# One VectorE operation a step in the wide waves, and three pieces of work moved between GpSimd, ScalarE and VectorE

## The chip, the cores and the metric

The kernel runs on one core of a Trainium2 chip. The metric is the device time of one execution in microseconds (us). A core has five engines with queues of their own: TensorE (PE) multiplies matrices into PSUM, VectorE (DVE) and ScalarE (ACT) compute on SBUF and PSUM, GpSimd (POOL) computes on SBUF, and SyncE (SP) issues nearly all DMAs here.[...]

## The reference

A block of three residual stages over x, 2048 tokens by 1024 channels in fp32. The middle stage convolves along the channel axis with a kernel that is built from a state-space model; the first and the last are the same gated feed-forward with weights of 4 bits:

```python
def _dequant(qweight, scales, qzeros, g_idx):   # groups of 128 rows
    ...
    return (w.astype(scales.dtype) - z[g_idx].astype(scales.dtype)) * s

x = L0_attn_u
x = x + 0.5 * _L0_ffn_ref(_layernorm(x, axis=-1), ...)   # silu(x@Wg) * (x@Wu) @ Wd
x = x + _L0_attn_ref(_layernorm(x, axis=-1), ...)        # y = causal conv(x, K) + D*x
x = x + 0.5 * _L0_ffn_ref(_layernorm(x, axis=-1), ...)
```

Wg and Wu are 1024 x 2752, Wd is 2752 x 1024; the 2752 inner channels are 21 tiles of 128 and a half tile of 64.

## The kernel before

**Jobs.** The tokens form four blocks of 512. A feed-forward of one block is a job; there are eight, numbered 0 to 7: `JOBS = [(0, 1), (1, 1), (0, 3), (1, 3), (2, 1), (3, 1), (2, 3), (3, 3)]`, each a block and a stage (1 the first feed-forward, 3 the last). A job has an up stage of 64 steps and a down stage of 44 steps.

**Up stage** (`gate_up`). A step is a wave of output tiles and one group of 128 input rows. Waves 0 to 4 are wide: three tiles of Wg and three of Wu, six units, steps 0 to 39. Waves 5 to 7 are narrow: four units in steps 40 to 55, and four and the half tile's unit in steps 56 to 63. A unit is one PSUM bank of 128 x 512 and takes two matmuls a step (L744), one with the low part of x (fp16, `xTl`) and one with the high part (`xTh`), in the same int8 weights cast to fp32r. After each step the bank is multiplied by the ratio of two groups' scales (`rat`), in place: even units on ScalarE (L714), odd ones on VectorE (L716), with some of unit 1's on ScalarE in jobs 0 and 1. The next step's matmuls on that bank wait for this. At the end of a wave, `gated` takes silu on ScalarE (L771), the product on VectorE (L774), and the high and low parts of h on GpSimd (L776, L778).

**Down stage** (`down`). The same for Wd, two halves of 22 steps, four banks (`po`), matmuls on L813. The half tile of 64 rows comes last in a half, at step 21; `gated_half` makes it: h of it stands in partitions 64 to 127, its high part stays there and its low part goes to partitions 0 to 63 of the same tile `hb`. `split` inside it is a generator of two GpSimd operations (L793, L795), which hooks pull at down steps 1 and 2.

**Hooks.** Everything else is attached to steps: `at(up, s, f)` and `at(dn, d, f)` call f when step s or d is written. Which step an instruction is written in, and its dependences, are what the Tile scheduler starts from; it then orders each engine's queue by its own estimate of times. `in_order_of_writing(f, engines)` pins the instructions of f, on the named engines, behind what was written on them before. `in_pieces` spreads the yields of a generator over a list of steps, pinned on VectorE; the last step takes all that is left.

**Preparing the next job.** While a job runs, the x of the next one gets its moments (`moments`, L187 and L188: two statistics of 512 columns and one aggregation for each of four tiles of 128 tokens), an inverse square root by three Newton rounds (`guess`, `deviations`, L195 to L213), and its normalization. From job 1 on, the normalization is `normalize` (L257), in place in x, eight pieces of 512 columns; in the down stage GpSimd splits x into parts and DMAs turn them. In jobs 3 and 4 the next x comes fresh from the input, so its moments lie there: all of them are written at up step 44, the Newton rounds at 45. In jobs 2, 5 and 6 the next x has just been convolved in the same job and saved to HBM (`save`, L1449, up step 28), and its moments are at 27. In jobs 2 to 6 the normalizations are written at up steps 46, 48, 50 and so on to 60. Job 1 prepares later and isn't touched by the change, and job 0 prepares job 1's x in its down stage in another way.

**Job 0** makes the int8 weights as it goes. For wave w, VectorE splits packed words into bytes in six pieces (L567, L569, L571), GpSimd copies eight int8 rows sets (L600), SP writes each to HBM (L601), and the weights of a step are read back (L676, four steps ahead) and cast three steps ahead, on GpSimd (L692) or, for some steps of job 0, on ScalarE (L690). `first_weights` sets the steps: wave 2's split starts at up step 3, with the fetch of wave 3's words and zero points three steps later.

**The opening.** Block 0's x is turned by TensorE, one chunk of 128 channels at a time (`first_turn`); chunk c is what step g = c of each wave needs. Chunks 0 to 4 go straight from PSUM: ScalarE casts the high part (L1589), VectorE subtracts for the low part (L1590). Chunks 5 to 7 are copied to SBUF by ScalarE (L1593), and GpSimd makes both parts (L1594, L1595).

Of the kernel before, what the change touches and what calls it, by code (L numbers as in the profile page):

```python
# [9 lines left out]
F32 = mybir.dt.float32  # L10
# [8 lines left out]
ALU = mybir.AluOpType  # L19
AX = mybir.AxisListType  # L20
ET = mybir.EngineType
# [20 lines left out]
LIFT = 2.0**20  # L42
# [13 lines left out]
def macaron_s4_kernel(  # L56
# [31 lines left out]
    nc = tc.nc  # L88
# [52 lines left out]
    def in_order_of_writing(f, *engines):  # L141

        start = len(nc.cur_bb.bb.instructions)
        got = f()
        written = list(nc.cur_bb.bb.instructions)
        for e in engines:
            last = next((i for i in reversed(written[:start]) if i.engine == e), None)
            for ins in written[start:]:
                if ins.engine == e:
                    if last is not None:  # L150
                        tc.add_manual_dep(
                            ins,
                            last.name,
                            mybir.DependencyInfo(
                                mybir.DependencyClass.NoSync, mybir.DependencyReason.DATA
                            ),
                            reason="order of writing",
                        )
                    last = ins
        return got  # L160
# [15 lines left out]
    def moments(b, k):  # L176
        for _ in moments_by_tile(b, k):
            pass

    def moments_by_tile(b, k):  # L180

        name = f"{b}_{k}"
        stats = small.tile([P, NT, 2, 6], F32, tag="stats", name=f"stats_{name}")
        mv = small.tile([P, NT, 2], F32, tag="mv", name=f"mv_{name}")
        for t in range(NT):
            for i in range(2):
                nc.vector.bn_stats(stats[:, t, i, :], x[b][t][:, bass.ts(i, 512)])  # L187
            nc.vector.bn_aggr(mv[:, t, :], stats[:, t, :, :].rearrange("p a s -> p (a s)"))  # L188
            yield
        guess(b, k, mv)  # L190
# [383 lines left out]
    def split(w):  # L574
        raw, z = packed[w]
        even = t4(f"even_{w}").bitcast(I32)[:, : width_of(w)]
        return signed_bytes(w, raw, even, z)
# [57 lines left out]
    def first_weights(up, dn, at):  # L635

        for w in range(1, len(WAVES)):
            s0 = (0, 3, 8 * w - 15)[min(w, 3) - 1]  # L640
            steps = (0, 1, 2, 2, 3, 3) if w == 1 else range(6)
            in_pieces(at, [(up, s0 + d) for d in steps], lambda w=w: split(w))
            copies = {1: (2, 2, 3, 3, 3, 3, 3, 3), 2: (3, 3, 4, 4, 6, 6, 7, 7)}
            if 1 < w < len(WAVES) - 1:
                both = lambda w=w: (fetch(w + 1), fetch_zeros(w + 1))
                at(up, s0 + 3, lambda both=both: in_order_of_writing(both, ET.SP))
            for k, d in zip((0, 2, 4, 6, 1, 3, 5, 7), copies.get(w, (3, 3, 4, 5, 6, 6, 7, 8))):
                at(up, s0 + d, lambda w=w, k=k: dequantize(w, k))
        s0 = len(STEPS) - 12
        when = lambda n: (up, s0 + n) if n < 12 else (dn, (5 * (n - 12)) // 6)  # L650
        for n in range(6 * 8):
            k, j = divmod(n, 8)
            a, rt = divmod(k, 3)
            if j == 0:
                at(*when(max(0, n - 7)), lambda a=a, rt=rt: fetch_down(a, rt))
                steps = [when(max(0, n - d)) for d in (4, 3, 3, 2, 1, 0)]
                in_pieces(at, steps, lambda a=a, rt=rt: split_down(a, rt))
            at(*when(n), lambda a=a, rt=rt, j=j: dequantize_down(a, rt, j))
# [122 lines left out]
    def gated_half(j, p):  # L781

        last = rat[:, 2 * WIDE, GK - 1 :]
        low, high = slice(0, HALF), slice(HALF, P)
        g = gpool.tile([P, TB], F32, tag="g", name=f"g_{j}_half")
        nc.scalar.activation(g[high], p[low], AF.Silu, scale=last[low])
        hf = hfpool.tile([P, TB], F32, tag="hf", name=f"hf_{j}_half")
        nc.vector.scalar_tensor_tensor(hf[high], p[high], last[high], g[high], ALU.mult, ALU.mult)
        both = hpool.tile([P, TB], F32R, tag="h", name=f"hb_{j}")
        h[WIDE] = (both,)  # L790

        def split():
            nc.gpsimd.tensor_copy(both[high], hf[high])  # L793
            yield
            nc.gpsimd.tensor_tensor(both[low], hf[high], both[high].bitcast(F32), ALU.subtract)  # L795

        half_split[j] = split()

    half_split = {}
    yT = {}  # L800
# [607 lines left out]
    def fast():  # L1408
        for j, (b, k) in enumerate(JOBS):
            prev = JOBS[j - 1] if j else None  # L1410
            after = JOBS[j + 1] if j + 1 < len(JOBS) else None
            up, dn = {}, {}

            def at(hooks, s, f):
                hooks.setdefault(s, []).append(f)
# [65 lines left out]
            if after:  # L1481
                ab, ak = after
                if ak == 1:
                    at(up, 55 if j == 0 else 6, lambda: load_x(ab, rows_of(u, ab)))
                    if j == 0:
                        steps = [(dn, d) for d in range(3, 8)]
                        in_pieces(at, steps, lambda: moments_by_tile(ab, 1))
                        newton = lambda: deviations(ab, 1, LIFT)
                        at(dn, 8, lambda: in_order_of_writing(newton, ET.DVE))
                    else:  # L1490
                        both = lambda: moments(ab, 1)
                        at(up, 44, lambda: in_order_of_writing(both, ET.DVE))
                        at(up, 45, lambda: deviations(ab, 1, LIFT))
                an = {}

                pool = j == 0

                def anorm(t):
                    an[t] = normalized(ab, t)

                o = 9 if j == 0 else 0
                turns = {}

                def turning(t):
                    if t not in turns:
                        turns[t] = [], []
                        turns[t] += (turn_by_dma(ab, t, turns[t][1]),)
                    rest = turns[t][1] or turns[t][2:]
                    next(rest[0], None)

                for t in range(NT if j else 0):
                    late = (12, 13) if t == NT - 1 else (13, 17)
                    for half in range(2):
                        piece = lambda t=t, half=half: normalize(ab, t, half)
                        piece = lambda piece=piece: in_order_of_writing(piece, ET.DVE)
                        at(*((dn, 3 * t + half) if j == 1 else (up, 46 + 4 * t + 2 * half)), piece)
                    for d in (1, 2, 3, 5, 6, 7, 9) + late:
                        piece = lambda t=t: turning(t)
                        piece = lambda piece=piece: in_order_of_writing(piece, ET.Pool, ET.SP)
                        at(dn, 2 + 9 * t + d, piece)  # L1520
                for t in range(0 if j else NT):
                    at(dn, o + 1 + 4 * t, lambda t=t: anorm(t))
                    at(dn, o + 2 + 4 * t, lambda t=t: turn(ab, t, an[t][:, :512], 0, by_pool=pool))
                    at(dn, o + 4 + 4 * t, lambda t=t: turn(ab, t, an[t][:, 512:], 1, by_pool=pool))
            for d in (1, 2):
                piece = lambda j=j: next(half_split[j], None)
                at(dn, d, lambda piece=piece: in_order_of_writing(piece, ET.Pool))
            o, gap = (27, 3) if j == 0 else (21, 4)
# [5 lines left out]
        b = JOBS[-1][0]  # L1534
# [41 lines left out]
    def first_turn(c):  # L1576

        if c == 0:
            pieces[0] = [
                xtpool.tile([P, NC, TB], dt, tag=f"xT{w}", name=f"xT{w}_0_1")  # L1580
                for w, dt in (("h", F32R), ("l", F16))
            ]
        hi, lo = (a[:, c, :] for a in pieces[0])
        ps = bank(f"pt_0_1_{c}")
        for t in range(NT):
            src = first[t, c // 4][:, bass.ts(c % 4, P)]
            nc.tensor.transpose(ps[:, bass.ts(t, P)], src, ident)
        if c < 5:
            nc.scalar.copy(hi, ps)  # L1589
            nc.vector.tensor_tensor(lo, ps, hi.bitcast(F32), ALU.subtract)  # L1590
        else:
            both = gpool.tile([P, TB], F32, tag="g", name=f"turn_0_1_{c}")
            nc.scalar.copy(both, ps)  # L1593
            nc.gpsimd.tensor_copy(hi, both)  # L1594
            nc.gpsimd.tensor_tensor(lo, both, hi.bitcast(F32), ALU.subtract)  # L1595
# [144 lines left out]
```

## Time and profile before

| | us |
|---|---|
| median of 3 runs | 2117.07 |
| lowest and highest | 2114.55, 2117.93 |
| the profiled execution | 2120.81 |
| its span, first to last instruction | 2118.6 |
| TensorE busy | 2065.1 |
| VectorE busy | 1674.5 |
| ScalarE busy | 1398.4 |
| GpSimd busy | 1298.0 |

In the profile, a group is named by its line in the kernel, its engine and its operation, with the tile that it writes and those that it reads. In an answer on waits, a row says which engine's instruction waited for which other, the total in us, how often, and the longest. In the chain, a row is a start in us from the span's begin, a length, and the engine and line that held the chain. In a timeline, a row is a start, a length, and a run of equal instructions with its count; brackets hold the engine's idle time before it and what ended it. The granted clock of TensorE was 0.995 of full speed over the span.

### The profile page before, as it was taken

To read this page: it belongs to the slowest core of one execution; us is meant where nothing else is said; L and a number is where in the kernel's file an instruction comes from. 1 tells how busy PE (TensorE), PEld (TensorE's weight loads), DVE (VectorE), ACT (ScalarE), POOL (GpSimd) and SP (SyncE) were. 2 spreads that over 40 slices of the span, in tenths; PEclk is the share of its full clock that TensorE was granted. 3 is DMA by queue.
4 is the path that set the end of the run, shared out by engine and by line. 5 is a ranking of instruction groups with operands and counts; after the bars stand their busy time and mean duration, and the time that the engine had idled before them with its cause. 6 is when DMAs were issued, how large, how long until landed. Compare 5 with 4: busy or idle time off the path is not lost.

```text
span 2118.6 us, 30223 instructions
## 1 busy us (share of the span) xinstructions
PE 2065.1 (97%) x9556; PEld 1410.2 (67%) x9556; DVE 1674.5 (79%) x2741; ACT 1398.4 (66%) x2185; POOL 1298.0 (61%) x1694
## 2 busy tenths in 40 slices
PE   5999899999999999999999999999999999999997
PEld 3555675677867568665776568676686766866576
DVE  8987978678788777778777787877878778777776
ACT  6777678646654776676767766546766467666775
POOL 5876747656744568455856468454684446845541
PEclk9999999999999999999999999999999999999999
DMA  4424322112511126211441115111151111531111
GB/s 136 125 84 142 98 71 57 36 54 54 128 39 53 31 52 164 76 35 33 110 146 35 32 42 132 37 51 40 36 137 39 53 37 35 132 127 36 33 36 58
DMA packets 239143, 151.02 MB, mean 71 GB/s; under 512 B 98683, under 2 KB 226532, under 8 KB 238974
## 3 DMA queue, kind: packets, MB, share of 16 engines
q1 hardware_dynamic: 237958, 147.12, 24.7%
q8 instruction: 78, 1.28, 0.3%
q10 hardware_dynamic: 728, 1.29, 0.2%
q14 instruction: 91, 0.75, 0.1%
q0 software_dynamic: 288, 0.59, 0.1%
HBM read 104.45 MB, written 25.50 MB: 61 GB/s over the span
## 4 chain that ended last, share of the span: by engine, by line
PE 90%; DVE 5%; POOL 2%; issue 1%; ACT 1%; DMA 1%; SPq 0%; DVEq 0%; POOLq 0%; ACTq 0%
PE pg L744 54%; PE po L813 28%; PE pc L1139 3%; DVE pg L716 2%; PE pb L835 1%; PE pb L1139 1%; PE st L228 1%; DVE po L716 0%; POOL q L600 0%; DMA b<-wq 0%; DVE x L257 0%; ACT pg L714 0%; DVE rawd L571 0%; DVE rawd L569 0%; DVE hf L774 0%
## 5 line engine op out<-in xcount | busy, mean ns | idle before, releaser
L714 ACT ACTIVATE pg<-pg,rat 128x512 f32<-128x512 f32 x1240 | 786.7, 660 | 431.2 <-PE pg L744 429.8
L716 DVE TENSOR_TENSOR pg<-pg,rat 128x512 f32<-128x512 f32 x1168 | 775.8, 693 | 171.6 <-PE pg L744 166.4
L744 PE MATMUL pg<-xTh,w_up 128*128 128x512 f32 x2752 | 855.9, 438 | 4.7 <-DVE pg L716 1.9
L744 PE MATMUL pg<-xTl,w_up 128*128 128x512 f16 x2752 | 725.7, 382 | 11.7 <-POOL w_up L692 5.5
L692 POOL CAST w_up<-b 128x768 fp32r<-128x768 int8 (+2 forms) x490 | 377.1, 776 | 512.3 <-PE pg L744 407.7
L744 PEld LDWEIGHTS pg<-xTh,w_up 128*128 128x128 f32 x2752 | 519.4, 189 | 181.3 <-DVE pg L716 13.9
L714 ACT ACTIVATE po<-po,ratd 128x512 f32<-128x512 f32 x660 | 432.4, 661 | 176.0 <-PE po L813 175.6
L813 PE MATMUL po<-hl,w_down 128*128 128x512 f32 x1344 | 534.0, 399 | 9.0 <-DVE po L716 8.4
L716 DVE TENSOR_TENSOR po<-po,ratd 128x512 f32<-128x512 f32 x620 | 430.3, 698 | 119.2 <-PE po L813 115.0
L813 PE MATMUL po<-hh,w_down 128*128 128x512 f32 x1344 | 523.5, 392 | 0.0
L744 PEld LDWEIGHTS <-w_up 128*128 128x128 bf16 x2752 | 228.2, 99 | 336.9 <-issue 158.9
L692 POOL CAST w_down<-bd 128x512 fp32r<-128x512 int8 x352 | 217.5, 620 | 171.9 <-PE po L813 96.5
L813 PEld LDWEIGHTS po<-hl,w_down 128*128 128x128 f32 x1344 | 252.6, 188 | 80.0 <-DVE po L716 19.0
L813 PEld LDWEIGHTS po<-hh,w_down 128*128 128x128 f32 x1344 | 253.6, 189 | 49.4
L778 POOL TENSOR_TENSOR hl<-hf,hh 128x512 fp32r<-128x512 f32 x168 | 217.8, 1296 | 8.3
L774 DVE SCALAR_TENSOR_TENSOR hf<-pg,rat,g 128x512 f32<-128x512 f32 x168 | 123.1, 748 | 49.5 <-ACT g L771 40.6
L771 ACT ACTIVATE g<-pg,rat 128x512 f32<-128x512 f32 x168 | 110.5, 686 | 49.0 <-PE pg L744 32.7
L776 POOL CAST hh<-hf 128x512 fp32r<-128x512 f32 x168 | 106.5, 634 | 58.2 <-PE pg L744 31.0
L283 POOL TENSOR_TENSOR lo<-x,hi 128x512 f16<-128x512 f32 x48 | 62.0, 1291 | 0.0
L187 DVE BATCH_NORM_STATS2 stats<-x 128x6 f32<-128x512 f32 x88 | 58.5, 676 | 0.5
L281 POOL TENSOR_TENSOR mid<-hi,top 128x512 bf16<-128x512 f32 x48 | 56.2, 1171 | 0.0
L297 POOL TENSOR_TENSOR xTh<-turned 128x512 fp32r<-128x512 bf16 x48 | 55.9, 1164 | 0.0
(214 smaller groups left out, 1113.7 us busy)
## 6 DMA issues: line engine op xcount, KB each, us to landing
b<-wq SPq DMA_DIRECT2D x319, 96.0 KB
bd<-wdq SPq DMA_DIRECT2D x336, 64.0 KB
x<-in_L_attn_u_dram SPq DMA_DIRECT2D x30, 512.0 KB
b<-wq SPq DMA_DIRECT2D x128, 64.0 KB
xs<-x SPq DMA_DIRECT2D x16, 512.0 KB
x<-xs SPq DMA_DIRECT2D x16, 512.0 KB
out_dram<-x SPq DMA_DIRECT2D x16, 512.0 KB
b<-wq SPq DMA_DIRECT2D x64, 80.0 KB
```

What stands on the lines that cost most here:

```text
L187: nc.vector.bn_stats(stats[:, t, i, :], x[b][t][:, bass.ts(i, 512)])
L283: nc.gpsimd.tensor_tensor(lo[:, own], n[:, own], hi[:, own].bitcast(F32), ALU.subtract)
L692: nc.gpsimd.tensor_copy(t, b)
L714: nc.scalar.activation(dst, src, AF.Copy, scale=sc)
L716: nc.vector.tensor_tensor(dst, src, sc.to_broadcast([P, TB]), ALU.mult)
L744: nc.tensor.matmul(p, weights, (lo, hi)[k][:, g, :], start=(g == 0 and not done), stop=(g == GK - 1 and done), skip_group_check=True,)
L771: nc.scalar.activation(g, pg, AF.Silu, scale=rat[:, 2 * f, GK - 1 :])
L774: nc.vector.scalar_tensor_tensor(hf, pu, last, g, ALU.mult, ALU.mult)
L776: nc.gpsimd.tensor_copy(hi, hf)
L778: nc.gpsimd.tensor_tensor(lo, hf, hi.bitcast(F32), ALU.subtract)
L813: nc.tensor.matmul(ps[c], w[:, bass.ts(c, P)], part, start=(f == 0 and k == 0), stop=(f == NF - 1), skip_group_check=True,)
L1139: nc.tensor.matmul(dst, lhsT, rhs, start=start, stop=stop, skip_group_check=True)
```

## The change

- In jobs 3 and 4 the moments are written in nine pieces, one statistic each, at up steps 18 to 26, and the Newton rounds at step 28, pinned on VectorE. `moments_by_tile` yields between a tile's two statistics for this.
- In jobs 2 to 6 the eight normalizations are written at up steps 31 to 38, one a step.
- Job 0's half tile is split on VectorE, where `gated_half` is written; other jobs keep GpSimd and the two hooks.
- Chunks 6 and 7 of the opening go the way of chunks 0 to 4; chunk 5 keeps GpSimd.
- Wave 2's split, int8 copies and the fetch of wave 3 in job 0 are one step later.

```diff
-    def moments_by_tile(b, k):
+    def moments_by_tile(b, k, halves=False):
...
                 nc.vector.bn_stats(stats[:, t, i, :], x[b][t][:, bass.ts(i, 512)])
+                if halves and i == 0:
+                    yield
...
-            s0 = (0, 3, 8 * w - 15)[min(w, 3) - 1]
+            s0 = (0, 4, 8 * w - 15)[min(w, 3) - 1]
...
-        def split():
-            nc.gpsimd.tensor_copy(both[high], hf[high])
-            yield
-            nc.gpsimd.tensor_tensor(both[low], hf[high], both[high].bitcast(F32), ALU.subtract)
-
-        half_split[j] = split()
+        def split(e):
+            e.tensor_copy(both[high], hf[high])
+            yield
+            e.tensor_tensor(both[low], hf[high], both[high].bitcast(F32), ALU.subtract)
+
+        half_split[j] = split(nc.gpsimd if j else nc.vector)
+        if j == 0:
+            for _ in half_split[j]:
+                pass
...
-                        both = lambda: moments(ab, 1)
-                        at(up, 44, lambda: in_order_of_writing(both, ET.DVE))
-                        at(up, 45, lambda: deviations(ab, 1, LIFT))
+                        steps = [(up, s) for s in range(18, 27)]
+                        in_pieces(at, steps, lambda: moments_by_tile(ab, 1, halves=True))
+                        newton = lambda: deviations(ab, 1, LIFT)
+                        at(up, 28, lambda: in_order_of_writing(newton, ET.DVE))
...
-                        at(*((dn, 3 * t + half) if j == 1 else (up, 46 + 4 * t + 2 * half)), piece)
+                        at(*((dn, 3 * t + half) if j == 1 else (up, 31 + 2 * t + half)), piece)
...
-            for d in (1, 2):
+            for d in (1, 2) if j else ():
...
-        if c < 5:
+        if c != 5:
             nc.scalar.copy(hi, ps)
             nc.vector.tensor_tensor(lo, ps, hi.bitcast(F32), ALU.subtract)
```

## The prediction

> **What bounds the kernel now.** I read the busy shares first, then the chain of work that ended last, then the waits and the order of work inside the stretches that the change touches.
>
> ```profile
> PE 2065.1 (97%) x9556; PEld 1410.2 (67%) x9556; DVE 1674.5 (79%) x2741; ACT 1398.4 (66%) x2185; POOL 1298.0 (61%) x1694
> ...
> PE 90%; DVE 5%; POOL 2%; issue 1%; ACT 1%; DMA 1%; SPq 0%; DVEq 0%; POOLq 0%; ACTq 0%
> ```
>
> TensorE carries 90% of the chain. What an edit off TensorE can win lies in the other tenth: places where TensorE waits. The pace without waits is seen in the last job (job 7), which has nothing to prepare for a next one. In the chain in order of time (start, length, count of matmuls):
>
> ```profile
> 858.83 115.30 PE pg L744 x509
> ...
> 1010.23 46.70 PE po L813 x204
> ...
> 1877.63 147.73 PE pg L744 x652
> ```
>
> 652 matmuls in 147.73 us are 0.2266 us each, so a step of a wide wave (12 matmuls) takes 2.72 us and one of a narrow wave (8) 1.81 us. Job 3 keeps that pace for 509 matmuls, up to 974.13, and reaches its down stage at 1010.23: 151.40 us for what job 7 does in 147.73. **Job 3 loses 3.67 us, all of it in the narrow waves.** Job 4 runs from 1100.73 to 1252.19, 151.46 us: 3.73 us lost. VectorE's timeline in job 3 shows why:
>
> ```profile
> 966.99 1.28 DVE L187 BATCH_NORM_STATS2 stats<-x 128x6 f32<-128x512 f32 x2
> 968.18 0.68 DVE L716 TENSOR_TENSOR pg<-pg,rat 128x512 f32<-128x512 f32 x1
> ...
> 979.92 0.85 DVE L212 SCALAR_TENSOR_TENSOR r<-e,r 128x4 f32<-128x4 f32 x1
> ...
> 987.42 2.40 DVE L257 TENSOR_SCALAR x<-x,mv,r 128x512 f32<-128x512 f32 x4
> ```
>
> Two statistics, then one rescaling of PSUM (L716), then two more; later four normalizations in a row, 2.40 us without a rescaling, though a step is 1.81 us. TensorE needs each rescaled bank in the next step. In a wide wave VectorE idles instead, 0.46 + 0.25 us of each step's 2.72:
>
> ```profile
> 866.55 1.30 DVE L716 TENSOR_TENSOR pg<-pg,rat 128x512 f32<-128x512 f32 x2 [0.46 <-PE pg L744]
> 868.10 0.70 DVE L716 TENSOR_TENSOR pg<-pg,rat 128x512 f32<-128x512 f32 x1 [0.25 <-PE pg L744]
> ```
>
> The other stretch is the start of job 0. TensorE's waits between 20 and 72 us, and GpSimd's order there:
>
> ```profile
> PE pg L744 <- POOL xTl L1595: 3.2, 1, 3.2
> PE pg L744 <- POOL w_up L692: 3.2, 2, 2.5
> ...
> 47.28 1.26 POOL L1595 TENSOR_TENSOR xTl<-turn,xTh 128x512 f16<-128x512 f32 x1
> 48.49 0.61 POOL L1594 CAST xTh<-turn 128x512 fp32r<-128x512 f32 x1
> 49.18 1.39 POOL L1595 TENSOR_TENSOR xTl<-turn,xTh 128x512 f16<-128x512 f32 x1
> 50.51 3.46 POOL L600 COPY q<-even 128x768 int8<-128x768 int8 x4
> 53.92 1.54 POOL L692 CAST w_up<-b 128x768 fp32r<-128x768 int8 x1
> ```
>
> Step 6 waits 3.16 us for chunk 6's low part, which ends at 48.54; step 8 waits 2.45 us for its weights, cast at 53.92 behind four int8 copies of the second wave; step 11 waits 0.71 us the same way.
>
> [...]L716's mean here is 693. [...]L257 has a median of 539 ns. [...]L1595's median is 1.39 us, the same subtraction on VectorE (L1590) 0.68. [...]in this trace the same cast of 768 columns (L692) takes 0.83 us, and 1.54 at 53.92 while VectorE runs a two-input operation.
>
> **The change part by part.**
>
> *Jobs 3 and 4.* The eight statistics (0.68 us), four aggregations, three seeds and ten Newton operations leave steps 44 to 51 for steps 18 to 28, one statistic a step; eight normalizations go from steps 46 to 60 to steps 31 to 38. The built order has one large operation behind every three rescalings, and TensorE's order in the narrow waves becomes regular, as job 7's. It removes 3.67 + 3.73 = 7.4 us. What it adds in the wide waves: a statistic holds VectorE 0.60 us (start to start) and a normalization 0.46, against 0.71 idle, so nothing reaches TensorE. The cover is known to work: in job 0, from 84.3 to 111.5, a splitting operation of 0.5 to 1.4 us sits in most wide steps, VectorE is busy 24.73 of 27.20 us, and TensorE is busy for 27.14. The tiny Newton operations are different: they run one behind the other, some hold 0.7 us, and they now come in about three steps. I charge 0.3 us a job (bounds 0 and 1.5). Data is there: this x is issued at 833.8 to 839.3, 60 us before step 18. Sum: **-6.8** (-7.4 to -4.4).
>
> *Jobs 2, 5 and 6.* Only their normalizations move. Matmul counts at job 7's pace give losses of about 1.1 (690 to 768.33), 0.8 (1445 to 1519.61) and 1.0 us (1715 to 1787.11), each uncertain by a matmul. I take 0.7 each: **-2.1** (-2.9 to 0). The normalization overwrites x, so it must follow the save (L1449); job 2 issues its four saves at 626.0, 643.9, 661.8 and 681.1, and step 31 starts near 695.6 by the count of matmuls, tile 3's turn at 711: 30 us or more each.
>
> *Opening.* Chunks 6 and 7 cost ScalarE the same one copy (0.60 us); GpSimd loses 2 x (0.61 + 1.3) = 3.8 us; VectorE gets 2 x 0.60 held. The low part of chunk 6 is then ready near 41.5, so step 6 could start at 45.3. But VectorE is gapless from 34.75 to 52.0, and in the new order the scale inverses (about 2.5 us), chunk 7's subtraction (0.6) and the wave-2 add (1.1 to 1.5) still stand ahead of step 5's rescaling of unit 3, which puts it near 49.5. So most of the 3.16 us turns into a wait for VectorE. The 2.45 is different: wave 1's last int8 copy ends about 0.6 us earlier (46.7 for 47.3), its write and the reload followed each other in 1.6 and about 2 us, and the cast now stands directly behind: ready near 51.5 for 55.46. TensorE, held to about 50 and running the half steps in between, passes that point near 52, some 3.5 us ahead; step 11's 0.71 goes too, its cast now preceding the high parts of h. I take 3.5 and lose 0.5 of it on the way: **-3.0** (-6.3 to 0).
>
> Moved with it: wave 2's six splits one step later, its eight int8 copies and writes, four fetches of wave 3 on SP (0.36 to 0.61 us of issue each) and the loads behind them. Wave 1's load for step 11 now precedes those fetches. Behind the later writes waits step 16's weight load: before, the last write was issued at 69.36, the load at 71.69, the cast ended at 76.3, step 16 began at 81.5. Of those 5.2 us the earlier TensorE takes about 3.5; about 2 are left, since GpSimd is also earlier. I charge nothing; without that cover the lead is lost, which is the lower bound.
>
> *Half chunk of job 0.* GpSimd loses 0.95 + 1.32 us at 207.65 to 210.8, VectorE gains a 64x512 copy (bounded by L257's 0.54) and a subtraction (0.69), about 1.1 held. There TensorE waits for VectorE:
>
> ```profile
> 206.40 1.74 DVE L569 TENSOR_TENSOR rawd<-rawd,zd 88x1024 uint16<-88x1024 uint16 x1
> ...
> 210.29 0.50 PE L813 MATMUL po<-hl,w_down 128*128 128x512 f32 x1 [2.09 <-DVE po L716]
> ```
>
> In the new order one rescaling (unit 1) comes before that add, the other still behind the whole block. So the wait splits and the added 1.1 us eats part: **-0.7** (-2.1 to +0.7).
>
> **Sum.** -6.8 - 2.1 - 3.0 - 0.7 = -12.6 us. The profiled execution took 2120.81 us (span 2118.6, 2.2 around it): 2108.2. It lies 3.74 above the median of 2117.07, so against the median 2104.5; I give **2105.0**.
>
> **Rivals.**
> *1. VectorE swallows the opening.* The release of GpSimd meets a gapless VectorE, whose two extra subtractions delay the rescalings; or step 16's load comes late. Then the opening gives 0: 2117.1 - 9.6 = 2107.5. For it: no VectorE gap from 34.75 to 52.0. Against: the wait for the step-8 cast was GpSimd's own.
> *2. The pieces move and the stalls with them.* The scheduler has placed the operations, but at the wave ends (steps 23/24, 31/32) products and a new wave's rescalings compete; half the jobs' gain goes and the opening gives none: 2117.1 - 4 = 2113. Against: VectorE waits for ScalarE there, 4.0 us in five waits in 858 to 958.
> *3. Slower: no room in the wide waves.* Per job 3 and 4, 8 x 0.60 + 8 x 0.46 + about 3 us of small operations are 11.5 us; with 8 x 0.46 in three jobs, 34 us of VectorE work moves. If banks came round so tightly that over 38% of it showed on TensorE, the 12.6 us are used up; at 60% the kernel takes about 2125. It decides when an operation delays a rescaling by more than the 0.71 us of idle. Against: job 0's stretch, where larger pieces cost nothing.
> *4. Not done.* The order could be undone by scheduling; the built order shows it is not.
>
> **How the numbers follow.** Forecast case 0.52, rival 1 0.26, rival 2 0.13, rival 3 0.09, rival 4 0. All upper bounds together give 18.7 us (2098.4), all lower ones 3.7 (2113.4); the far ends need all at once, so 2099.5 to 2113.5. A measurement here tells about 0.2%, 4.2 us. The forecast and rival 1 are faster by more; rival 2 lies on the line, half of it faster. Faster 0.84, same 0.07, slower 0.09.
>
> **What would show it.** Jobs 3 and 4 should take about 148 us over the 652 matmuls, with L187 and L257 alone between rescalings in wide steps and no lone rescalings of VectorE in the chain of the narrow waves. TensorE's wait for L1595 should be gone, replaced by a shorter one for L716 near 48 to 50; the step-8 cast should end near 51.5 and step 16 start near 78. Wrong would be: gaps of TensorE for L716 between steps 18 and 38, a wait for POOL at step 16, or a wait of L257 for a save.

## The result, and the profile after

The changed kernel takes **2103.72 us** (median of 4 runs, 2102.25 to 2104.70) against 2116.74 for the kernel before (4 runs beside it, 2114.55 to 2117.93): ratio 0.9939, 95% interval 0.9922 to 0.9956, 13.0 us less. Forecast were 2105.0 and 12.6 less. The total came out; its parts did not all do so, and that is what the rest is about.

The profiled execution took 2103.03 us, 0.7 under its median; that of before lay 4.1 above its own. So the two traces differ by 17.8 us where the medians differ by 13.0. In the changed kernel the line numbers are a few higher: L744 is now L746, L716 is L718, L257 is L259, L813 is L818.

The busy shares and the shares of the chain (the page's first and fourth part) of the changed kernel:

```profile
PE 2056.2 (98%) x9556; PEld 1409.2 (67%) x9556; DVE 1674.5 (80%) x2745; ACT 1398.3 (67%) x2185; POOL 1290.8 (61%) x1688
...
PE 92%; DVE 4%; ACT 1%; DMA 1%; issue 1%; POOL 0%; SPq 0%; ACTq 0%; DVEq 0%; POOLq 0%
```

VectorE's work is the same, 1674.5 us; GpSimd has 7 us less. TensorE carries 92% of the chain for 90. The chain in order of time shows where (start, length, matmuls):

```profile
847.81 78.30 PE pg L746 x347
...
929.72 66.34 PE pg L746 x291
996.06 46.70 PE po L818 x204
...
1860.17 147.72 PE pg L746 x652
```

In this chain, job 3's up stage runs from 847.81 to 996.06: 148.25 us, against 151.40 before and 147.72 in job 7. The narrow waves now go through without a break (291 matmuls in 66.34 us, 0.228 us each). What is left, 0.53 us, lies mostly between the two rows: 3.61 us for 14 matmuls, 3.17 at job 7's pace, and the chain leaves TensorE there, near 927. VectorE's timeline in a wide wave of job 3 (start, length, count; idle time before in brackets) has the form that the prediction asked for, one statistic behind three rescalings:

```profile
889.22 0.68 DVE L187 BATCH_NORM_STATS2 stats<-x 128x6 f32<-128x512 f32 x1
889.82 0.68 DVE L718 TENSOR_TENSOR pg<-pg,rat 128x512 f32<-128x512 f32 x1
890.72 1.30 DVE L718 TENSOR_TENSOR pg<-pg,rat 128x512 f32<-128x512 f32 x2 [0.22 <-PE pg L746]
891.93 0.68 DVE L187 BATCH_NORM_STATS2 stats<-x 128x6 f32<-128x512 f32 x1
```

The rescalings still wait for TensorE (0.22 us) and not the other way round. Near 927, at the first step of wave 4 (step 32), it is different. VectorE, and then GpSimd at the same time:

```profile
925.33 2.34 DVE L776 SCALAR_TENSOR_TENSOR hf<-pg,rat,g 128x512 f32<-128x512 f32 x3 [0.36 <-ACT g L773]
927.58 1.48 DVE L259 TENSOR_SCALAR x<-x,mv,r 128x512 f32<-128x512 f32 x1
928.98 1.88 DVE L718 TENSOR_TENSOR pg<-pg,rat 128x512 f32<-128x512 f32 x3
```

```profile
926.70 0.83 POOL L694 CAST w_up<-b 128x768 fp32r<-128x768 int8 x1
927.49 1.28 POOL L780 TENSOR_TENSOR hl<-hf,hh 128x512 fp32r<-128x512 f32 x1
```

One normalization (L259) takes 1.48 us and ends 0.29 us after GpSimd's subtraction does; of the other seven of this job six take 0.54 and the next one 0.94. The first rescaling of the new wave stands behind it, and TensorE waits. This costs 0.6 us in each of jobs 2 to 6.

The opening, TensorE's waits between 20 and 72 us (in total, times, longest), and the cast that step 8 waits for:

```profile
PE pg L746 <- DVE pg L718: 3.1, 2, 2.7
PE pg L746 <- POOL w_up L694: 2.4, 2, 1.4
```

```profile
49.42 0.83 POOL L694 CAST w_up<-b 128x768 fp32r<-128x768 int8 x1 [3.71 <-DMA b<-wq]
```

The wait of 3.2 us for chunk 6's low part is gone and the cast ends at 50.25 for 55.46 before. A new wait has come: 2.7 us for VectorE. In the chain, TensorE stands behind eight conversions of job 0's zero points for the down stage. They took 3.08 us in the trace before and held up less. First that trace, then the changed kernel, with GpSimd beside it:

```profile
69.60 3.08 DVE L339 TENSOR_SCALAR zi<-zq 84x32 int32<-84x32 int32 x8
```

```profile
66.52 4.65 DVE L341 TENSOR_SCALAR zi<-zq 84x32 int32<-84x32 int32 x8
```

```profile
67.05 0.82 POOL L694 CAST w_up<-b 128x768 fp32r<-128x768 int8 x1
67.83 3.13 POOL L602 COPY q<-even 128x768 int8<-128x768 int8 x4
```

Such a conversion takes 0.18 us by itself. One that takes longer (0.57 to 0.88 us here) ends 0.05 to 0.06 us after one of GpSimd's operations. In the trace before this happened to four of the eight, in the changed kernel to six.

By parts, from the starts of the steps in the two traces:

| part | predicted | after less before, us |
|---|---|---|
| jobs 3 and 4, up stage | -6.8 | -3.1 and -3.2 |
| jobs 2, 5 and 6, up stage | -2.1 | -0.2, 0.0 and -0.2 |
| job 0, start of step 6; 8; 11; 16 | step 16: -3.0 | -3.8; -5.0; -5.6; -1.0 |
| job 0, steps 53 to 56 | 0 | -3.5 |
| job 0, rest of the up stage | 0 | -0.8 |
| job 0, down stage | -0.7 | -5.0 |
| job 1, up stage | 0 | -0.6 |

The -3.5 is not the change's. The profiled run of before waited 2.34 us at step 53 for weights that a DMA brought late and lost 3.8 us in steps 53 and 54; the five other profiles with the old opening or one of its two edits lose 0.2 to 0.7 at step 53 (the eight with both edits 0.3 to 2.7). It is about the size of the 4.1 us by which that run lay over its median.

### The profile page after: what moved, and what is told of

Its sections match the earlier page's. It is cut to its first block, busy times and chain, and to the rows that moved or that the text cites. A ratio compares the mean times of both kernels' runs of the same rounds, so it can differ in the third digit from the quotient of the medians.

```text
span 2101.2 us, 30226 instructions
## 1 busy us (share of the span) xinstructions
PE 2056.2 (98%) x9556; PEld 1409.2 (67%) x9556; DVE 1674.5 (80%) x2745; ACT 1398.3 (67%) x2185; POOL 1290.8 (61%) x1688
## 3 DMA queue, kind: packets, MB, share of 16 engines
q8 instruction: 78, 1.28, 0.3%
## 4 chain that ended last, share of the span: by engine, by line
PE 92%; DVE 4%; ACT 1%; DMA 1%; issue 1%; POOL 0%; SPq 0%; ACTq 0%; DVEq 0%; POOLq 0%
PE pg L746 57%; PE po L818 29%; PE pc L1144 3%; PE pb L840 1%; PE pb L1144 1%; DVE pg L718 1%; PE st L230 1%; DVE po L718 0%; DMA b<-wq 0%; DVE rawd L569 0%; DVE x L259 0%; DVE xn L223 0%; DMA x<-in_L_attn_u_dram 0%; POOL q L602 0%; DVE rawd L571 0%
## 5 line engine op out<-in xcount | busy, mean ns | idle before, releaser
L716 ACT ACTIVATE pg<-pg,rat 128x512 f32<-128x512 f32 x1240 | 786.7, 660 | 415.5 <-PE pg L746 414.4
L718 DVE TENSOR_TENSOR pg<-pg,rat 128x512 f32<-128x512 f32 x1168 | 776.5, 693 | 159.6 <-PE pg L746 153.6
L746 PE MATMUL pg<-xTh,w_up 128*128 128x512 f32 x2752 | 843.0, 435 | 3.8 <-DVE pg L718 3.1
L746 PE MATMUL pg<-xTl,w_up 128*128 128x512 f16 x2752 | 719.0, 382 | 7.2 <-DVE pg L718 4.0
L746 PEld LDWEIGHTS pg<-xTh,w_up 128*128 128x128 f32 x2752 | 518.4, 189 | 173.7 <-DVE pg L718 13.8
L716 ACT ACTIVATE po<-po,ratd 128x512 f32<-128x512 f32 x660 | 431.7, 661 | 170.4 <-PE po L818 170.3
L818 PE MATMUL po<-hl,w_down 128*128 128x512 f32 x1344 | 532.2, 398 | 6.9 <-DVE po L718 5.5
L718 DVE TENSOR_TENSOR po<-po,ratd 128x512 f32<-128x512 f32 x620 | 430.4, 698 | 115.8 <-PE po L818 111.5
L818 PE MATMUL po<-hh,w_down 128*128 128x512 f32 x1344 | 522.2, 391 | 0.0
L746 PEld LDWEIGHTS <-w_up 128*128 128x128 bf16 x2752 | 228.5, 99 | 331.1 <-issue 154.7
L818 PEld LDWEIGHTS po<-hl,w_down 128*128 128x128 f32 x1344 | 251.6, 188 | 78.5 <-DVE po L718 15.7
L818 PEld LDWEIGHTS po<-hh,w_down 128*128 128x128 f32 x1344 | 252.6, 188 | 48.7
```

The lines of the kernel that those rows point to most:

```text
L716: nc.scalar.activation(dst, src, AF.Copy, scale=sc)
L718: nc.vector.tensor_tensor(dst, src, sc.to_broadcast([P, TB]), ALU.mult)
L746: nc.tensor.matmul(p, weights, (lo, hi)[k][:, g, :], start=(g == 0 and not done), stop=(g == GK - 1 and done), skip_group_check=True,)
L818: nc.tensor.matmul(ps[c], w[:, bass.ts(c, P)], part, start=(f == 0 and k == 0), stop=(f == NF - 1), skip_group_check=True,)
```

## The experiments

The first three do one part alone, on the kernel before. The ratio and the gain are taken against runs of the kernel before that were made beside each (medians 2114.82 to 2115.75).

**Jobs alone.** Only the moments and normalizations (the first, fifth and sixth hunk of the diff).

> Only the moments of jobs 3 and 4 and the normalizations of jobs 2 to 6 are moved; opening, wave 2 and half chunk stay as before. Theory (the job part is independent of job 0): jobs 3 and 4 are 3.1 to 3.2 us shorter in the up stage, jobs 2, 5 and 6 0 to 0.2 us, so about -6.7 us in all, 0.9968 of before. Rival (the gain of the jobs comes from what job 0 hands on): less than half of that.

Measured: 2107.66 us (5 runs), ratio 0.9961, interval 0.9948 to 0.9975. Up stages of jobs 3 and 4: -3.46 and -3.18 us; of jobs 2, 5 and 6: -0.05, +0.04, -0.06. Job 0 is written as before here, and is 4.1 us shorter than in the profile before, 3.5 of it in steps 53 to 56: the control for the table above. So this part is worth some 6.7 us by the trace, 8 by the medians.

**Opening alone.** Only chunks 6 and 7 and the later second wave.

> Only chunks 6 and 7 on ScalarE and VectorE and wave 2 one step later. Theory (the opening's lead of 5 us at step 11 is taken back at steps 13 to 16, where VectorE's zero-point block stands): step 16 starts about 1 us earlier than before, whole kernel -1 to -2 us. Rival (the lead survives, and the rest of job 0 shows it): -4 to -6 us.

Measured: 2112.92 (21 runs), ratio 0.9986, 0.9979 to 0.9992: 2.8 us gained, between the two expectations. The theory's reason does not hold here: the lead over the kernel before is 5.8 us at step 11 and still 4.6 at step 16. The block of zero points took 3.10 us in this kernel, as before, and not 4.65.

**Half chunk alone.**

> Only job 0's half chunk on VectorE. Theory (GpSimd's 2.3 us were on the path of the down stage's start): job 0's down stage 1.5 to 3 us shorter, whole kernel the same. Rival (VectorE's added 1.1 us eats it): 0 to -0.7 us.

Measured: 2109.87 (13 runs), ratio 0.9975, 0.9967 to 0.9983: 5.3 us by the ratio, 5.9 by the medians. Both theories were too small. Job 0's down stage is 4.7 us shorter: 1.1 up to step 4, where the wait for VectorE split as predicted, and 3.4 at steps 23 and 24, fifty microseconds after the edit. There, in the kernel before, a conversion of job 0's weights takes 2.58 us on VectorE:

```profile
261.89 2.58 DVE L571 TENSOR_SCALAR rawd<-rawd 88x1024 uint16<-88x1024 uint16 x1
```

```profile
261.79 0.61 POOL L692 CAST w_down<-bd 128x512 fp32r<-128x512 int8 x1
262.36 1.27 POOL L248 TENSOR_TENSOR xTl<-turn,xTh 128x512 f16<-128x512 f32 x1
263.58 0.61 POOL L692 CAST w_down<-bd 128x512 fp32r<-128x512 int8 x1
264.53 0.61 POOL L629 COPY qd<-rawd 88x512 int8<-88x512 int8 x1 [0.34 <-DVE rawd L571]
```

It began beside three GpSimd operations without a gap and ended at 264.47, 0.28 us after the third; two rescalings behind it kept TensorE waiting 0.7 and 1.9 us. In the kernel with the half chunk moved the same operation stands in the same place of VectorE's order:

```profile
255.04 0.83 DVE L571 TENSOR_SCALAR rawd<-rawd 88x1024 uint16<-88x1024 uint16 x1
```

**Half chunk on VectorE, with spare work on GpSimd.** Is it GpSimd's release, or the order?

```diff
+        def spare():
+            unused = hf[low].bitcast(F32R)
+            nc.gpsimd.tensor_copy(unused, hf[high])
+            yield
+            nc.gpsimd.tensor_tensor(unused, hf[high], both[high].bitcast(F32), ALU.subtract)
...
+            for _ in split(nc.vector):
+                pass
+            half_split[j] = spare()
```

> The kernel before with job 0's half chunk split on VectorE as in the changed kernel, while GpSimd still does the two operations at down steps 1 and 2, of the same shapes, into the unused half of the tile hf, for nobody. It tells apart what the half chunk's gain of 4.7 us in job 0's down stage (half_alone) comes from. Theory: GpSimd's release does it; its later work falls otherwise against VectorE's conversions[...] (2.58 us for an operation of 0.83). With the spare operations GpSimd's order is nearly that of before, so the gain at down steps 23 to 25 (3.5 us) goes and only the split wait at steps 2 and 3 (1.4 us) stays: the down stage 0.5 to 1.5 us shorter than before, about 2114.5. Rival: the place of the subtraction on VectorE does it, ahead of the rescalings instead of behind a wait for GpSimd: the stage stays 4.7 us shorter, about 2110.

Measured: 2111.70 (8 runs), ratio 0.9976, 0.9965 to 0.9986; down stage again 4.7 us shorter, and the conversion takes

```profile
255.95 0.79 DVE L571 TENSOR_SCALAR rawd<-rawd 88x1024 uint16<-88x1024 uint16 x1
```

The theory fell: the gain doesn't need GpSimd to be relieved. It goes with the order. In the built order VectorE differs only in the first twenty operations of the stage, but GpSimd's pieces (parts of x, copies of `qd`, casts of `w_down`) stand otherwise in places, most of all between steps 16 and 26. All five profiles with the old order (before, jobs, opening, chunks and second wave alone) have the operation at 2.58 or 2.59 us and lose 5.1 to 5.2 us at steps 23 and 24; all nine with the half chunk on VectorE lose 1.2 to 1.8. That the reordered pieces cause it is argued from this; which of them decides was not tried.

**No normalization at step 32.**

```diff
-                        at(*(... (up, 31 + 2 * t + half)), piece)
+                        at(*(... (up, (30, 31, 33, 34, 35, 36, 37, 38)[2 * t + half])), piece)
```

> The changed kernel with the normalizations at steps 30, 31, 33 to 38 instead of 31 to 38: none at the first step of a wave. Theory (the 0.6 us that jobs 2 to 6 lose at step 32 come from the normalization between the products and the new wave's first rescaling): the loss goes in all five jobs, 3 us less than the changed kernel, about -16 us against before. Rival (the wave end stalls whenever normalizations are near it, the one ahead of the products included): the loss stays at step 31 or 32, no difference from the changed kernel.

Measured: **2099.71** (5 runs), ratio 0.9924, 0.9910 to 0.9937. The chain of this kernel runs through the up stages of jobs 3 and 4 without a break, at job 7's pace (147.74 in this run):

```profile
848.49 147.71 PE pg L746 x652
...
1086.70 147.73 PE pg L746 x652
```

Jobs 2 to 6 are 0.54, 0.54, 0.56, 0.65 and 0.58 us shorter than in the changed kernel, 2.9 us together, as the theory said. It is the fastest median of all; the interval overlaps that of the changed kernel, so that it is faster rests on the trace. A normalization is still drawn out in this kernel, at step 33, and TensorE has no wait between 918 and 940:

```profile
930.50 1.15 DVE L259 TENSOR_SCALAR x<-x,mv,r 128x512 f32<-128x512 f32 x1
```

So being drawn out was not enough (1.15 us here without a wait of TensorE); the loss of 0.6 us came where it stood ahead of a new wave's first rescaling.

**A statistic at step 32.** What makes step 32 costly: the place or the operation?

```diff
-                        steps = [(up, s) for s in range(18, 27)]
+                        steps = [(up, s) for s in (18, 19, 20, 21, 22, 23, 32, 33, 34)]
-                        at(up, 28, lambda: in_order_of_writing(newton, ET.DVE))
+                        at(up, 35, lambda: in_order_of_writing(newton, ET.DVE))
-                        at(*(... (up, 31 + 2 * t + half)), piece)
+                        at(*(... (up, 36 + t)), piece)
```

> The changed kernel, with one statistic of jobs 3 and 4 (0.60 us held) in the place at step 32 that a normalization (0.46 held, 1.48 measured there) has in the changed kernel; the last statistic and the aggregation follow at 33, the seed at 34, Newton at 35, and the normalizations of jobs 2 to 6 go two a step at 36 to 39. Theory: the loss of 0.6 us at step 32 comes from the normalization being drawn out to 1.48 us while GpSimd splits the products; a statistic is not drawn out (0.60 to 0.69 everywhere so far), so steps 31 to 33 of jobs 2 to 6 lose nothing. Rival: any operation of VectorE between the products and the first rescaling of the new wave delays it: jobs 3 and 4 still lose 0.6 us or more at step 32, jobs 2, 5 and 6 nothing.

Measured: 2104.10 (one run). VectorE in job 3, in the very place of the 1.48 us above, with the same GpSimd operations beside it (its subtraction at 927.84 for 1.28 us):

```profile
927.95 0.68 DVE L187 BATCH_NORM_STATS2 stats<-x 128x6 f32<-128x512 f32 x1
928.55 1.88 DVE L718 TENSOR_TENSOR pg<-pg,rat 128x512 f32<-128x512 f32 x3
```

No loss at steps 31 to 34 of jobs 3 and 4, nor in jobs 2, 5 and 6, where nothing stands at step 32 in this kernel. The theory holds: the place alone did not cost it; an operation that was drawn out in that place did (1.48 us against 0.68). The doubled normalizations cost about 0.3 us at step 41 in jobs 3 to 6, and jobs 3 and 4 lose 0.7 at step 37.

**Wide wave or one a step.** Two kernels separate the halves of the edit. One writes the moments of jobs 3 and 4 in one block, but at step 18; the other spreads them one a step, but over steps 40 to 48 (Newton at 50, the normalizations of jobs 2 to 6 at 53 to 60).

```diff
-                        in_pieces(at, steps, lambda: moments_by_tile(ab, 1, halves=True))
+                        both = lambda: moments(ab, 1)
+                        at(up, 18, lambda: in_order_of_writing(both, ET.DVE))
```

```diff
-                        steps = [(up, s) for s in range(18, 27)]
+                        steps = [(up, s) for s in range(40, 49)]
```

> The changed kernel, with the moments of jobs 3 and 4 in one block from up step 18 (two statistics and one aggregation between one rescaling and the next, as the kernel before has them in its narrow waves) and their Newton steps at 28. It tells apart which half of the edit matters: the wide wave or one operation a step. If the wide wave alone matters, jobs 3 and 4 stay as in the changed kernel (0.6 us lost at step 32 only): 2103.7. If one operation a step matters too: four blocks of about 1.4 us and four rescalings make 8.4 us of VectorE for work that takes TensorE 3.6, so 2 to 4 us are lost in steps 18 to 22 of either job: 2108 to 2112.

> The changed kernel, with one operation a step as it has it, but in the narrow waves: moments of jobs 3 and 4 at steps 40 to 48, Newton steps at 50, normalizations of jobs 2 to 6 at steps 53 to 60. If one operation a step alone matters, nothing is lost, not even the 0.6 us at step 32: jobs 2 to 6 each gain 0.6, 2100.7. If the wide wave matters: a narrow step leaves VectorE about 0.4 us beside two rescalings, a statistic holds it 0.60 and a normalization 0.46, so eight statistics lose some 1.6 us, the Newton steps about 1 and the normalizations up to 0.5: 2.5 to 3 us lost in jobs 3 and 4 and up to 0.5 in jobs 2, 5 and 6, about 2107.

Measured: in a lump 2102.20 (4 runs), ratio 0.9941, 0.9923 to 0.9958; jobs 3 and 4 -3.07 and -3.09 us against before, as in the changed kernel, with nothing lost at steps 18 to 31. Narrow: 2104.11 (4 runs), ratio 0.9954, 0.9936 to 0.9972; jobs 3 and 4 only -2.07 and -1.17, with losses of 0.3 to 0.4 us at step 41 and of 1.1 and 1.6 over steps 49 to 51, and the 0.6 us at step 32 gone in all five jobs. **The wide wave is what counts**; one operation a step adds nothing measurable there (in the lump kernel the scheduler also laid TensorE's matmuls beside the block in another order), and in the narrow waves it takes away a third to somewhat over a half of the loss.

**Zero points spread.** Does the block of 4.65 us take the opening's lead?

```diff
-                at(up, 12, lambda: in_order_of_writing(zeros, ET.DVE, ET.SP))
+                in_pieces(at, [(up, s) for s in (15, 16, 18, 20, 22, 23, 24, 26, 28)], zeros)
```

> The changed kernel, with job 0's zero points for the down stage computed in nine pieces at up steps 15 to 28 instead of in one block at step 12. Theory: in the changed kernel the opening's lead over the kernel before is 5.6 us at step 11 and 1.0 at step 16 because this block of eight small conversions and their followers (4.65 us on VectorE from 66.5) now falls where TensorE is ahead and holds back the rescalings of steps 13 and 14. Spread out, the excess of steps 12 to 14 (3.4 + 1.6 us) should fall to about 1.5, step 16 should start about 4.5 us ahead of the kernel before, and the time should be about 3 us under the changed kernel's 2103.7: 2100.7. Rival: the lead is given back by whatever is late next (the second wave's weights through GpSimd, step 16's load); then the lead at step 16 stays near 1 us and the time stays at 2103.7.

> The changed kernel with both repairs: normalizations at steps 30, 31, 33 to 38 (none at step 32) and the zero points spread over steps 15 to 28. If the two losses are independent the gains add: 4.0 us from step 32 (2099.7 was measured) and 3 us from the opening, 2096.7. If the opening's lead is lost in another way it stays at 2099.7.

Measured: 2103.81 (6 runs), ratio 0.9948, 0.9934 to 0.9963, and with step 32 mended as well 2101.43 (6 runs), 0.9939, 0.9925 to 0.9952. The block's loss at steps 13 and 14 goes (5.0 us to 0.6; the lead at step 14 is 5.0), but step 16 then waits. TensorE, and ScalarE a little earlier, in the kernel with the zero points spread:

```profile
80.00 0.38 PE L757 MATMUL pg<-xTl,w_up 128*128 128x512 f16 x1 [3.31 <-ACT g L784]
```

```profile
77.80 1.56 ACT L703 CAST w_up<-b 128x768 fp32r<-128x768 int8 x2 [3.57 <-DMA b<-wq]
79.27 1.84 ACT L784 ACTIVATE g<-pg,rat 128x512 f32<-128x512 f32 x3
```

TensorE waits for the silu (L784) that frees its bank. The silu stands in ScalarE's queue behind two weight casts, which waited 3.57 us for weights read back from HBM. Step 16's own weights had been cast by 73.47; by the order of the casts these two belong to steps 17 and 18. So the second wave's weights, written and read back, are late next, and hold step 16 through ScalarE's queue. The rival was right and nothing was won.

The other profiles bear on the block's length. In the twelve kernels that keep it in one block it takes either 3.08 to 3.11 us, with four conversions drawn out, or 4.65, with six. Six of these kernels have both edits of the opening. Three of them have the long block, lose 5.0 to 5.1 us at steps 13 and 14 and lead by 1.0 to 2.0 at step 16; three have the short one, lose 2.2 to 3.6 and lead by 3.2 to 4.6. Up to step 16 all six have the same instructions in the same order on TensorE, VectorE, ScalarE and GpSimd. So the edits of the opening don't decide the length. In the trace before, four conversions that began within 0.01 us of the start of one of GpSimd's operations took 0.18 us; in the changed kernel five that began so took 0.87 to 0.88. What decides it was not shown. The changed kernel's profile shows the long block. Each kernel has one profile, so whether it would show the other in another execution is open.

**The opening's two edits, each alone.**

```diff
-        if c < 5:
+        if c != 5:
```

```diff
-            s0 = (0, 3, 8 * w - 15)[min(w, 3) - 1]
+            s0 = (0, 4, 8 * w - 15)[min(w, 3) - 1]
```

> The kernel before with only chunks 6 and 7 of the opening split on ScalarE and VectorE; the second wave's splits stay at step 3. By the prediction's working this removes the wait for the chunk's low part at step 6 (up to 3.2 us), but the weights of step 8 stay behind the second wave's copies on GpSimd, which itself has 3.8 us less to do. Step 8 should start 2 to 4 us ahead of the kernel before. Theory: the edit carries most of the opening's gain (2.8 us for both edits together): 2112.5 to 2114. Rival: without the shift of the second wave the wait only moves to step 8 and nothing is won: 2115.7.

> The kernel before with only the second wave's splits one step later (from step 4). Step 6 still waits for chunk 6's low part (3.2 us), the four int8 copies come behind the cast for step 8. Theory: the wait at step 8 (2.5 us) goes, and some 1 us is kept to step 16, about 2114.7. Rival: the two edits of the opening need each other; alone this one only makes the third wave's weights later: no gain or a loss of up to 2 us, 2115.7 to 2117.7.

Measured: chunks 2113.97 (21 runs), ratio 0.9990, 0.9983 to 0.9996, step 16 3.4 us ahead; second wave 2116.16 (13 runs), ratio 1.0002, 0.9993 to 1.0010, step 6 still waiting 3.7 us for the chunk. The chunks carry the gain; the later wave may add to it (1.6 us against 2.8 for both), but the intervals overlap.

## Why the prediction was right, point by point

- **Jobs 3 and 4: right** (-6.8 forecast, -6.3 measured). The wide waves take the statistics at no cost; the lump run shows even more room than the sum assumed. The 0.3 us a job charged for the Newton steps was misplaced: they cost nothing, and the 0.6 at step 32 was the cost. The step that failed is "a statistic holds VectorE 0.60 us (start to start) and a normalization 0.46, against 0.71 idle, so nothing reaches TensorE": true of the statistic, but the 0.46 was the time of an undisturbed normalization. The trace before held the warning: its median is 0.54 us, but 17 of its 48 normalizations took over 0.6, the longest 1.25.
- **Jobs 2, 5 and 6: mis-sized** (-2.1 forecast, -0.4 measured). The same term. Each job won its 0.7 in the narrow waves and lost 0.6 at step 32; without a normalization there the three are 0.75, 0.68 and 0.74 us shorter than before. Rival 2 had named the wave ends as the place, and spoke of products and rescalings; the runs put it down to one operation between them, where it is drawn out (1.48 us for 0.54). The prediction had noted a longer time beside the other engine for GpSimd's cast only (1.54 us for 0.83). In the fourteen traces 231 normalizations take over 0.6 us, and every one ends 0.28 to 0.29 us after one of GpSimd's operations, while a statistic in the same place took 0.68. Why a normalization ends there was not shown.
- **Opening: size right, path not** (-3.0 forecast; 2.8 timed alone; step 16 1.0 ahead in the changed kernel, 1.6 to 4.6 in the five other profiles with the same order there, against 0.0 to 0.9 in three with the old one). The step-8 cast came earlier than forecast (50.25 for 51.5). The wait for VectorE "near 49.5" that should have eaten the step-6 gain did not come: the rescaling of unit 3 starts at 47.27, and step 6 is 3.8 us ahead. The 0.5 us lost "on the way" became up to 4.6 in the changed kernel, first to the zero points at steps 13 and 14, a block that the prediction did not price; with that block spread, step 16 waits for the second wave's weights, through the casts of steps 17 and 18. There the prediction charged nothing and named step 16's own load as the risk, which was in time.
- **Half chunk: mis-sized** (-0.7 forecast, -4.7 and -5.0 in the down stage, -5.3 timed alone). The wait split as described (2.09 us before; after, two waits of 1.11 and 1.17 in other places), and steps 2 and 3 gained about 1. The other 3.4 us came at steps 23 and 24, where GpSimd's queue is ordered otherwise. The failed step is where the look ended: the built order was read around the edit, and not to the end of the stage.
- **The total** fits by luck, because errors of both signs met: 0.5 and 1.7 us less than forecast in the jobs, 4 more in the half chunk, about 1 less in the opening (2.6 us is the mean lead at step 16 of the six profiles, 0.5 that of the three controls). Timed alone, the parts gain 8, 3 and 5 to 6 us, 16 to 17 for 13.0 together; the intervals of the parts (some 2.8 us either way for the jobs, 1.4 for the opening, 1.7 for the half chunk) allow that, so an interaction isn't shown. Rival 3 fell, the wide waves had room. Of rival 1 a part came in the changed kernel, through other VectorE work than it named.

## What to carry to other kernels

Move an engine's side work to where that engine waits for the bottleneck, measured per step; in the wide waves here that mattered, and how finely it was spread did not. Before placing an operation ahead of a critical one, look at what its neighbour engine runs at that moment, and at the longest durations of its kind, not at the median alone. Where a block's operations end just behind those of such a neighbour (3.08 us for a block in one profile, 4.65 in another), read more than one profile before pricing it. When a scheduler reorders, compare the queues to the end of the stage: the largest effect of a small edit may be fifty microseconds on.

## What the runs showed of the hardware

- The same fp32 normalization of 512 columns takes 0.54 us, and 1.48 beside GpSimd's work (1.46 in job 4). All 231 that took over 0.6 us in the fourteen traces end 0.28 to 0.29 us after an operation of GpSimd's. A statistic in the same place takes 0.68, and none of the 92 in each trace takes over 0.70.
- A uint16 operation of 88x1024 takes 0.41 us at best and 2.58 beside three GpSimd operations without a gap, in five profiles of five. In the trace before it ended 0.28 us after the third of them, 0.83 after the second and 2.07 after the first.
- A conversion of 84x32 takes 0.18 us by itself. The ten of the two traces that took longer, 0.57 to 0.88, ended 0.05 to 0.06 us after one of GpSimd's copies or casts. Eight in a row took 3.08 us in the trace before, with four drawn out so, and 4.65 in the changed kernel's, with six.
- The weights of job 0's step 53, read back from HBM, came so that the step lost 0.2 to 3.0 us from profile to profile, more often over 1 us with the new opening (six of eight) than with the old. Whether the earlier start is given back there in part stays open; in one profile alone such a wait can pass for a gain or a loss of 3 us.
